# Three bias additions of an attention layer moved from GpSimd's arithmetic to accumulating DMAs

## The chip, the cores and the metric

The kernel runs on one core of a Trainium2 chip. That core has a matrix engine (TensorE, PE in the profile; its weight loads are shown apart as PEld), a vector engine (VectorE, DVE), an activation engine (ScalarE, ACT), a general engine (GpSimd, POOL) and SyncE (SP), which here only issues DMAs. Each engine works through its own queue of instructions in order, and waits on semaphores for the others. The metric is the device time of one execution in microseconds; the times below are the median and the extremes of three executions, and one further execution that the hardware profiler recorded.

## The reference, cut to what matters

The program is a network of two layers over x (32 batches of 512 nodes by 256 features) and an integer adjacency adj (32 x 512 x 512). Layer 0 is a graph convolution and a two-branch feed-forward part; the change does not touch it. Layer 1 is an attention over the graph (4 heads of 64) and a "slice token" mixer (8 heads, 64 slices), each with a layer norm ahead of it and a residual addition behind it:

```python
# attention, per batch; W (4, 256, 64)
h = einsum('bnd,hde->bhne', layernorm(x), W)
weight = leaky_relu(mask * (e_src + e_dst))        # one edge type that matters
weight = where(adj == 0, -1e9, weight)
dst = einsum('bhij,bhje->bhie', softmax(weight), h) + bias
out = relu(dst) + h
out = (out - mean) / sqrt(var + eps) * ln_gamma + ln_beta
x = x + out
# mixer, per batch
sw = softmax((xm @ W_slice.T + b_slice) / temp)    # 512 nodes x (8 heads x 64 slices)
st = einsum('bhnc,bhng->bhgc', fx, sw) / (sum of sw)
ot = state-space mixer over the 64 slice tokens (st)
x = x + einsum('bhgc,bhng->bhnc', ot, sw) @ out_w.T + out_b
```

The three biases of the change are `bias` of the attention (gnn_bias), `ln_beta` and `out_b`. All three are rows of 256 numbers, the same for every node.

## The kernel before, in words

Layer 0 runs first, up to about 2390 us of the span; layer 1 takes the rest, up to 4456 us. Layer 1 is one Python generator. For each batch the nodes lie as 128 partitions times NT = 4 node tiles, so a batch's x is a tile of 128 x 1024 numbers, 512 KB.

**Attention of a batch.** `prepare(b)` gathers x by four indirect DMAs on GpSimd's queue (L1154), builds the mask, normalises x into `xn` (statistics on VectorE L1126, L1127, the inverse root on GpSimd, the scaling on ScalarE L1133), and has GpSimd add beta to x (L1167). Then come the transposes of `xn` and, for each of the four node tiles t, a matmul into a PSUM bank `hp` (L1180). From that bank ScalarE makes `mine` (L1183), the exponential weight of each source node, kept as the 65th column of `hv` (L1184), `other` (L1185), and the copy `ht` of the values (L1186). After all four tiles GpSimd forms the values `hv = ht + abias` (L1189), VectorE multiplies them in place by the weight (L1202), and a small transpose `minep` (L1193) sends `mine` through DRAM to be spread over the partitions as `own` (DMAs at L1198 and L1200). `attention(b)` then forms the weights `att` on VectorE (L1213), multiplies them with `hv` on TensorE (`avp` L1249 for the values, `adp` L1254 for the sums of the weights), copies and transposes both back, and divides: `av = bp * rs` (L1275). Because the weight column sums to the divisor, a bias that is in every value comes out of the division unchanged.

`norm(b, av)` finishes a batch in three parts, which are resumed between the turns of the next batch's attention: first `av = max(av, 0) + ht` (L1290), the mean and its subtraction, and the squares on ScalarE; then the variance, GpSimd's power (L1300) and gamma; then the scaling by the inverse root and `x += av` (L1304).

**Mixer of a pair of batches.** `mixer(g)` takes GB = 2 batches. `slices(b, …)` normalises x again into `x4` (L1133), transposes it, has GpSimd add out_b to x (L1328), and for four node tiles makes logits `lgp` (L1335), their exponential `sw` on ScalarE (L1336) and the softmax on VectorE: times a constant (L1337), row sums (L1340), reciprocal (L1341), scaling (L1342). `yTp` (L1347) multiplies x4 with the finished `sw`, and `swp` (L1352) transposes `sw`. `tokens` and `scan` work on the 64 tokens of both batches. `unslice` multiplies back (`outp` L1567), VectorE adds to x (L1569) and SP stores it.

**What sets the order.** The attention of the batches ahead is woven into the mixer by a pace written by hand: each `yield` of the mixer pays credit (`PACE`, built from `TURNS + STEPS`), and for every whole credit the attention advances by one `yield`. Inside it, `prepare(b+1)` is woven into `attention(b)`, STEPS against TURNS. A scheduler then gives each engine its queue by its own costs and due times, so the order on an engine is not quite that of the program; the buffers (two of `hv`, `ht`, `other`; four PSUM banks called `any`, shared by hp, lgp, yTp, swp, outp and the rest) add waits of their own.

The lines that set it:

```python
PACE = 1.04 * GB * (TURNS + STEPS) / WANTED
...
if unfinished and i != 2:
    next(unfinished[0], None)
    yield
    if i > 2:
        unfinished.pop()
...
yield from woven(attention(b), TURNS - 4, nxt, STEPS)
```

Of the kernel before, what the change touches and what calls it, by code (L numbers as in the profile page):

```python
# [8 lines left out]
F32 = mybir.dt.float32  # L9
# [4 lines left out]
AF = mybir.ActivationFunctionType  # L14
# [5 lines left out]
P = 128  # L20
# [844 lines left out]
def layer1_plain(tc, ident, eps, x2s, ranks, adj, w, out, over, ps):  # L865
# [21 lines left out]
    HE = HO + 1  # L887
    AP = AH // 2
    TURNS = AP * NT + 6
    STEPS = 15  # L890
    WANTED = 68
    AHEAD = 3
    ATT = 2 * (AHEAD + 2) + AP + 1
# [7 lines left out]
    with ExitStack() as ctx:  # L901
# [39 lines left out]
            nc.vector.tensor_scalar(over[:, : 2 * AH], pn[:, : 2 * AH], SMALL, None, ALU.is_gt)  # L941
        yield
        edges = ctile("edges", [P, 2, B * NT])
        abias = const("abias", [P, AH * HO], w["gnn_bias"].rearrange("h e -> (h e)").partition_broadcast(P))
        gamma = const("gamma", [P, AH * HO], w["ln_gamma"].rearrange("h e -> (h e)").partition_broadcast(P))
        beta = const("beta", [P, AH * HO], w["ln_beta"].rearrange("h e -> (h e)").partition_broadcast(P))
        bfx = const("bfx", [P, KC, 1], w["b_fx"].rearrange("(k p o) -> p k o", p=P, o=1))
        bfx_eps = ctile("bfx_eps", [P, KC])
        nc.vector.tensor_scalar_mul(bfx_eps, bfx[:, :, 0], -1e-5)
        outb = const("outb", [P, D], w["out_b"].partition_broadcast(P))  # L950
        conv_w = const("conv_w", [P, KC, KW], w["hy_conv_w"][:DI].rearrange("(c p) k -> p c k", p=P))
        conv_b = const("conv_b", [P, KC], w["hy_conv_b"][:DI].rearrange("(c p) -> p c", p=P))
        bc_w = const("bc_w", [S, 2, KW], w["hy_conv_w"][DI:].rearrange("(c p) k -> p c k", p=S))
# [194 lines left out]
        def prepare(b):  # L1148

            while b >= AHEAD_X and b - AHEAD_X not in stored:  # L1150
                yield True
            xt = xs[b] = sb.tile([P, NT, D], F32, tag="x", name=f"x{b}", bufs=AHEAD_X)
            for t in range(NT):
                nc.gpsimd.indirect_dma_start(  # L1154
                    out=xt[:, t, :], out_offset=None, in_=x2s[b // SEG],
                    in_offset=bass.IndirectOffsetOnAxis(
                        ap=ranks[:, b * NT + t : b * NT + t + 1].bitcast(U32), axis=0))

            hv = sb.tile([P, NT, AH, HE], F32, tag="hv", name=f"hv{b}")
            xn = hv.rearrange("p t h e -> p (t h e)")[:, : NT * D].rearrange("p (t d) -> p t d", t=NT)  # L1160
            edged = masks(b) if b not in masked else range(3)
            for i, _ in enumerate(edged):
                if i < 3 or b not in masked:
                    yield
                if i == 2:
                    normed(xt, xn, f"c{b}")
                    nc.gpsimd.tensor_add(xt, xt, beta.unsqueeze(1).to_broadcast([P, NT, D]))  # L1167
                    yield
            mask = masked.pop(b)
            xnT = yield from turned(xn, "x3T", f"x3T{b}")  # L1170
            yield


            ht = sb.tile([P, NT, AH * HO], F32, tag="ht", name=f"ht{b}")
            other = sb.tile([P, NT, AH], F32, tag="other", name=f"other{b}")
            mine = sb.tile([P, AH, NT], F32, tag="mine", name=f"mine{b}")
            for t in range(NT):
                ph = psum("any", f"hp{b}_{t}")
                for c in range(DC):
                    nc.tensor.matmul(ph[:, : AH * (HO + 2)], xnT[:, c, t * P : (t + 1) * P], wa[:, c, :],  # L1180
                                     start=c == 0, stop=c == DC - 1)
                d = ph[:, AH * HO : AH * HO + AH]
                nc.scalar.activation(mine[:, :, t], ph[:, AH * (HO + 1) : AH * (HO + 2)], AF.Exp, scale=1.0 - SLOPE)  # L1183
                nc.scalar.activation(hv[:, t, :, HO], d, AF.Exp)  # L1184
                nc.scalar.activation(other[:, t, :], d, AF.Exp, scale=SLOPE - 1.0)  # L1185
                nc.scalar.copy(ht[:, t, :], ph[:, : AH * HO])  # L1186
                yield

            nc.gpsimd.tensor_add(hv[:, :, :, :HO], ht.rearrange("p t (h e) -> p t h e", h=AH),  # L1189
                                 abias.rearrange("p (h e) -> p h e", h=AH).unsqueeze(1).to_broadcast([P, NT, AH, HO]))  # L1190
            yield
            pt = psum("any", f"minep{b}")
            nc.tensor.transpose(pt[: AH * NT, :P], mine.rearrange("p h t -> p (h t)"), ident)  # L1193
            row = sb.tile([AH * NT, P], F32, tag="turned", name=f"turned{b}", bufs=1)
            nc.scalar.copy(row, pt[: AH * NT, :P])
            own_row = dr.tile([AH, N], F32, tag="own", name=f"ownd{b}")
            nc.sync.dma_start(own_row.rearrange("h (t p) -> (h t) p", p=P), row)
            own = [wide("own", f"own{b}_{h}", AH + 1) for h in range(AH)]  # L1198
            for h in range(AH):
                nc.sync.dma_start(own[h], own_row[h].partition_broadcast(P))  # L1200
            for t in range(NT):
                nc.vector.tensor_mul(hv[:, t, :, :HO], hv[:, t, :, :HO], hv[:, t, :, HO:].to_broadcast([P, AH, HO]))  # L1202
            ready[b] = mask, ht, hv, other, own
            yield

# [10 lines left out]
        def attention(b):  # L1216

            mask, ht, hv, other, own = ready[b]
            xt = xs[b]
            av = sb.tile([P, NT, AH, HO], F32, tag="av", name=f"av{b}", bufs=1)  # L1220
            turns = [(q, j) for j in range(NT) for q in range(AP)]

            def begin(b, n):
                q, j = turns[n]
                if (b, 2 * q, j) not in weighed:
                    weigh(b, q, j)

            def back(src, kind):

                dst = psum("pv", f"{kind}{b}")  # L1230
                for t in range(NT):
                    nc.tensor.transpose(dst[:, t * P : (t + 1) * P], src[:, t * P : (t + 1) * P], ident)
                return dst

            for n in range(AHEAD):
                begin(b, n)
            pv = [psum("pv", f"avp{b}_{q}") for q in range(AP)]
            for i, (q, j) in enumerate(turns):
                if i + AHEAD < len(turns):
                    begin(b, i + AHEAD)  # L1240
                elif b + 1 in ready:
                    begin(b + 1, i + AHEAD - len(turns))

                if q + 1 == AP:
                    ends = dict(start=j == 0, stop=j == NT - 1)
                    for p in range(AP):
                        for k in range(2 * HO // HW):
                            h, e = 2 * p + k * HW // HO, k * HW % HO
                            nc.tensor.matmul(pv[p][k * HW : (k + 1) * HW, :], hv[:, j, h, e : e + HW],  # L1249
                                             weighed[b, h, j], **ends)  # L1250
                    if j == 0:
                        pd = psum("pv", f"adp{b}")
                    for h in range(AH):
                        nc.tensor.matmul(pd[h * HW : (h + 1) * HW, :], hv[:, j, h, HO:].to_broadcast([P, HW]),  # L1254
                                         weighed.pop((b, h, j)), **ends)
                yield
                if unfinished and i != 2:
                    next(unfinished[0], None)
                    yield
                    if i > 2:  # L1260
                        unfinished.pop()
            dT = wide("att", f"adT{b}", ATT)
            nc.scalar.copy(dT, pd)
            vT = [wide("att", f"avT{b}_{q}", ATT) for q in range(AP)]
            for q in range(AP):
                nc.scalar.copy(vT[q], pv[q])
            yield
            dt = back(dT, "dp")
            rs = sb.tile([P, NT, AH], F32, tag="rs", name=f"rs{b}")
            nc.vector.tensor_scalar_max(rs, dt.rearrange("p (t h e) -> p t h e", t=NT, h=AH)[:, :, :, 0], 1e-30)  # L1270
            nc.vector.reciprocal(rs, rs)
            for q in range(AP):
                bt = back(vT[q], f"bp{q}_")
                heads = slice(2 * q, 2 * q + 2)
                nc.vector.tensor_mul(av[:, :, heads, :], bt.rearrange("p (t h e) -> p t h e", t=NT, h=2),  # L1275
                                     rs[:, :, heads].unsqueeze(3).to_broadcast([P, NT, 2, HO]))
                yield
            unfinished.append(norm(b, av))

        unfinished = []  # L1280
# [37 lines left out]
        def slices(b, j, yT, rn):  # L1318
# [6 lines left out]
            normed(xt, xn, f"d{b}")  # L1325
            yield 5
            xnT = yield from turned(xn, "x4T", f"x4T{b}", 1)
            nc.gpsimd.tensor_add(xt, xt, outb.unsqueeze(1).to_broadcast([P, NT, D]))  # L1328
            sw = sb.tile([P, NT, DI], F32, tag="sw", name=f"sw{b}", bufs=1)
            swT = sb.tile([P, KC, N], F32, tag="swT", name=f"swT{b}")  # L1330
            yield 2
# [908 lines left out]
```

## Time and profile before

| | us |
|---|---|
| median of three executions | 4460.33 |
| lowest, highest | 4456.45, 4473.15 |
| the profiled execution's own time | 4459.08 |
| its span | 4456.4 |
| TensorE busy in it | 3922.0 |
| VectorE busy | 3347.2 |
| ScalarE busy | 2291.6 |
| GpSimd busy | 1718.8 |
| mean granted TensorE clock (share of full speed) | 0.948 |

The profiled execution lies 2.7 us of time outside of its span (4459.08 − 4456.4). A group of instructions in the profile is written as line, engine, operation, out<-in, shape, count, then total busy time and the mean duration of one in nanoseconds, then the idle time of that engine just before them with what ended it. Times in waits are totals over the stretch asked for, with how often and the longest. In layer 1 a pair of batches takes 126.3 us between 2460 and 4230 us (14 pairs); there are 16 pairs.

### The profile page before, as it was taken

How to read it: one execution, taken by the hardware profiler on the slowest of the kernel's cores; microseconds unless marked ns; L12 is line 12 of the kernel's file. 1: busy time of each engine (PE TensorE's matmuls, PEld its weight loads, DVE VectorE, ACT ScalarE, POOL GpSimd, SP SyncE). 2: the span in 40 equal slices, each digit the busy share in tenths (PEclk: the TensorE clock that was granted, in tenths of full speed). 3: DMA queues.
4: the chain of work that ended last, by engine and by line, in shares of the span. 5: the costliest groups of instructions: out<-in, count | busy, mean ns of one | idle time of the engine just before them, and what ended most of it. 6: DMA issues, size and time to landing. Idle time of an engine off the chain costs nothing.

```text
span 4456.4 us, 57911 instructions
## 1 busy us (share of the span) xinstructions
PE 3922.0 (88%) x20311; PEld 2470.6 (55%) x20311; DVE 3347.2 (75%) x7008; ACT 2291.6 (51%) x4756; POOL 1718.8 (39%) x2036
## 2 busy tenths in 40 slices
PE   5568898899988999888997899999999999999987
PEld 4454565566656656545554455555555555555555
DVE  6668887897788987877766777767677877778763
ACT  3345565566564665556654544544545444454433
POOL 2357644664446644454314232332222232332220
PEclk8679999999999999989998999999999999999998
DMA  5546543664436543564422111111111111111100
GB/s 133 160 144 223 190 130 122 210 200 139 156 117 213 187 147 129 162 201 167 138 81 67 36 53 57 56 48 58 51 43 42 53 55 55 58 48 58 41 15 16
DMA packets 235107, 474.21 MB, mean 106 GB/s; under 512 B 38299, under 2 KB 114075, under 8 KB 234804
## 3 DMA queue, kind: packets, MB, share of 16 engines
q0 software_dynamic: 98688, 315.94, 22.2%
q1 hardware_dynamic: 136116, 154.46, 11.0%
q8 instruction: 162, 2.65, 0.2%
q14 instruction: 141, 1.16, 0.1%
HBM read 413.16 MB, written 57.16 MB: 106 GB/s over the span
## 4 chain that ended last, share of the span: by engine, by line
DVE 34%; PE 32%; DMA 11%; issue 9%; POOL 9%; ACT 5%; SPq 0%; POOLq 0%; DVEq 0%; ACTq 0%
DVE att L1213 5%; DVE acc L637 4%; PE clsp L623 3%; PE avp L1249 3%; PE po L652 3%; PE gatep L623 3%; DMA rows<-table,xs 2%; PE yTp L1347 2%; DVE sw L1337 2%; DVE sw L1342 2%; DVE best L598 2%; DMA rows<-table,tops 2%; DVE sst L1340 2%; DMA best<-table,xs 2%; PE xp L1400 1%
## 5 line engine op out<-in xcount | busy, mean ns | idle before, releaser
L623 PE MATMUL clsp<-xnT,wc 128*128 128x512 f32 x1024 | 520.8, 627 | 49.7 <-ACT cls L625 37.6
L623 PE MATMUL gatep<-xnT,wg 128*128 128x512 f32 x1024 | 499.8, 607 | 10.5 <-ACT gate L625 7.7
L652 PE MATMUL po<-wd,acc 128*128 128x256 f32 x2048 | 455.4, 381 | 6.1 <-DVE acc L641 3.8
L1213 DVE SCALAR_TENSOR_TENSOR att<-own,other,mask 128x512 f32<-128x512 f32 x512 | 392.9, 796 | 79.0 <-DMA own<-ownd 79.0
L652 PEld LDWEIGHTS po<-wd,acc 128*128 128x128 f32 x2048 | 388.3, 191 | 72.1 <-issue 9.2
L598 DVE SCALAR_TENSOR_TENSOR best<-rows,xs,best 128x1024 f32<-128x1024 f32 x212 | 274.4, 1295 | 121.9 <-ACT best L592 76.4
L637 DVE SCALAR_TENSOR_TENSOR acc<-past,fld,acc 128x512 f32<-128x512 f32 x448 | 345.7, 775 | 24.9 <-ACT past L636 16.9
L632 ACT ACTIVATE acc<-tz,fld 128x512 f32<-128x512 f32 x256 | 198.8, 777 | 269.3 <-PE tz L630 240.1
L623 PEld LDWEIGHTS gatep<-xnT,wg 128*128 128x128 f32 x1024 | 196.0, 196 | 252.3 <-issue 197.9
L636 ACT ACTIVATE past<-tz,fld 128x512 f32<-128x512 f32 x448 | 291.4, 693 | 68.1 <-DVE acc L637 66.6
L1347 PE MATMUL yTp<-sw,x 128*128 128x512 f32 x512 | 264.6, 655 | 64.3 <-DVE sw L1342 59.6
L595 POOL DMA_INDIRECT rows<-table,xs x212 | 249.5, 1177 | 171.6 <-DVE best L598 119.0
L1249 PE MATMUL avp<-att,hv 128*32 128x512 f32 x2048 | 298.9, 607 | 5.6 <-DVE att L1213 5.6
L623 PEld LDWEIGHTS clsp<-xnT,wc 128*128 128x128 f32 x1024 | 181.5, 198 | 188.1 <-issue 111.8
L434 PE MATMUL pm<-h,adj 128*128 128x258 f32 (+1 forms) x1024 | 181.2, 324 | 99.9 <-DVE keep L427 33.7
L1300 POOL TENSOR_TENSOR mu<-mu,eps 128x16 f32<-128x16 f32 x32 | 111.6, 3487 | 391.1 <-DVE mu L1299 391.0
L1335 PE MATMUL lgp<-wsl,x4T 128*128 128x512 f32 x512 | 242.8, 613 | 15.7 <-ACT sw L1336 6.8
L1154 POOL DMA_INDIRECT x<-x2s,ranks x128 | 135.9, 1062 | 298.1 <-DVE att L1213 148.1
L625 ACT ACTIVATE gate<-gatep,fld 128x512 f32<-128x512 f32 x256 | 175.5, 685 | 142.6 <-PE gatep L623 123.8
L553 POOL DMA_INDIRECT xs<-rows_of,order x128 | 156.1, 1219 | 221.5 <-DVE acc L637 100.8
L1567 PE MATMUL outp<-v,swT 128*128 128x256 f32 x1024 | 227.6, 381 | 0.0
L625 ACT ACTIVATE cls<-clsp,fld 128x512 f32<-128x512 f32 x256 | 176.1, 688 | 93.9 <-PE clsp L623 55.6
(599 smaller groups left out, 8978.1 us busy)
## 6 DMA issues: line engine op xcount, KB each, us to landing
adj<-in_adj POOLq DMA_DIRECT2D x128, 256.0 KB
ai<-in_adj SPq DMA_DIRECT2D x128, 256.0 KB
own<-ownd SPq DMA_DIRECT2D x128, 256.0 KB
rows_of<-keep SPq DMA_DIRECT2D x32, 550.0 KB
x<-in_x SPq DMA_DIRECT2D x32, 512.0 KB
x2s<-xs SPq DMA_DIRECT2D x32, 512.0 KB
out<-x SPq DMA_DIRECT2D x32, 512.0 KB
rows<-table,xs POOLq DMA_INDIRECT x212
```

Of the source, the lines that this page charges most:

```text
L595: nc.gpsimd.indirect_dma_start(out=row, out_offset=None, in_=table, in_offset=bass.IndirectOffsetOnAxis(ap=idxs[:, k : k + 1].bitcast(U32) ...
L598: nc.vector.scalar_tensor_tensor(m, row, vals[:, k : k + 1], m, ALU.add, ALU.max)
L623: nc.tensor.matmul(pf, wf[:, c, f * P : (f + 1) * P], xnT[:, c, :], start=c == 0, stop=c == DC - 1)
L625: nc.scalar.activation(o, pf, fn, bias=fld[:, f, bf : bf + 1], scale=1.0 if fn == AF.Gelu else 0.5)
L636: nc.scalar.activation(r, z, AF.Relu, bias=fld[:, f, AT + b : AT + b + 1])
L637: nc.vector.scalar_tensor_tensor(y, r, fld[:, f, CH + b : CH + b + 1], y, ALU.mult, ALU.add)
L652: nc.tensor.matmul(po[:, i, :], acc[f][:, t * P : (t + 1) * P], wd[:, f, :], start=f == 0, stop=f == FC - 1)
L1213: nc.vector.scalar_tensor_tensor(e, own[h], other[:, j, h : h + 1], mask[:, j, :], ALU.max, ALU.mult)
L1249: nc.tensor.matmul(pv[p][k * HW : (k + 1) * HW, :], hv[:, j, h, e : e + HW], weighed[b, h, j], **ends)
L1335: nc.tensor.matmul(pf, xnT[:, c, t * P : (t + 1) * P], wsl[:, c, :], start=c == 0, stop=c == DC - 1)
L1347: nc.tensor.matmul(py, xn[:, t, c * P : (c + 1) * P], sw[:, t, :], start=t == 0, stop=t == NT - 1)
L1567: nc.tensor.matmul(po[:, :D], swT[:, k, t * P : (t + 1) * P], v[:, k, :], start=k == 0, stop=k == KC - 1)
```

## The change

The three SBUF constants `abias`, `beta` and `outb` go. A DRAM tile `added` of three rows, each the bias row four times (4 KB), is filled by three DMAs on SP. `add_rows` issues from GpSimd's queue a DMA that reads one such row for each of the 128 partitions and adds it to the tile that stands there: 128 rows of 4 KB, 512 KB. It takes the place of GpSimd's additions of beta (L1167) and out_b (L1328). The attention's bias is no longer put into the values: right after ScalarE's exponential of a node tile (which now comes ahead of `mine`), VectorE multiplies the values straight from the PSUM bank by the weight and writes `hv` (after: L1191 and L1192), one tile at a time; the bias is accumulated onto the divided result `av` after the last division, and `norm` reads it after that. The yield behind the old L1189 goes (STEPS 14), and the three parts of `norm` run in turns 1, 2 and 4 where they ran in 0, 1 and 3.

```diff
-    STEPS = 15
+    STEPS = 14
...
-        abias = const("abias", [P, AH * HO], w["gnn_bias"].rearrange("h e -> (h e)").partition_broadcast(P))
+        added = dr.tile([3, NT, D], F32, tag="added", name="added", bufs=1)
+        for i, row in enumerate((w["gnn_bias"].rearrange("h e -> (h e)"), w["ln_beta"].rearrange("h e -> (h e)"),
+                                 w["out_b"])):
+            nc.sync.dma_start(added[i], row.partition_broadcast(NT))
+        added = added.rearrange("i t d -> i (t d)")
+        ABIAS, BETA, OUTB = range(3)
+
+        def add_rows(dst, i):
+
+            nc.gpsimd.dma_start(dst, added[i].partition_broadcast(P), accum_op=ALU.add)
+
...
-        beta = const("beta", [P, AH * HO], w["ln_beta"].rearrange("h e -> (h e)").partition_broadcast(P))
...
-        outb = const("outb", [P, D], w["out_b"].partition_broadcast(P))
...
                     normed(xt, xn, f"c{b}")
-                    nc.gpsimd.tensor_add(xt, xt, beta.unsqueeze(1).to_broadcast([P, NT, D]))
+                    add_rows(xt.rearrange("p t d -> p (t d)"), BETA)
                     yield
...
                 d = ph[:, AH * HO : AH * HO + AH]
+                nc.scalar.activation(hv[:, t, :, HO], d, AF.Exp)
+                nc.vector.tensor_mul(hv[:, t, :, :HO], ph[:, : AH * HO].rearrange("p (h e) -> p h e", h=AH),
+                                     hv[:, t, :, HO:].to_broadcast([P, AH, HO]))
                 nc.scalar.activation(mine[:, :, t], ph[:, AH * (HO + 1) : AH * (HO + 2)], AF.Exp, scale=1.0 - SLOPE)
-                nc.scalar.activation(hv[:, t, :, HO], d, AF.Exp)
                 nc.scalar.activation(other[:, t, :], d, AF.Exp, scale=SLOPE - 1.0)
                 nc.scalar.copy(ht[:, t, :], ph[:, : AH * HO])
                 yield
 
-            nc.gpsimd.tensor_add(hv[:, :, :, :HO], ht.rearrange("p t (h e) -> p t h e", h=AH),
-                                 abias.rearrange("p (h e) -> p h e", h=AH).unsqueeze(1).to_broadcast([P, NT, AH, HO]))
-            yield
             pt = psum("any", f"minep{b}")
...
-            for t in range(NT):
-                nc.vector.tensor_mul(hv[:, t, :, :HO], hv[:, t, :, :HO], hv[:, t, :, HO:].to_broadcast([P, AH, HO]))
             ready[b] = mask, ht, hv, other, own
             yield
...
-                if unfinished and i != 2:
+                if unfinished and i not in (0, 3):
                     next(unfinished[0], None)
                     yield
-                    if i > 2:
+                    if i > 3:
                         unfinished.pop()
...
                 yield
+
+            add_rows(av.rearrange("p t h e -> p (t h e)"), ABIAS)
             unfinished.append(norm(b, av))
...
             xnT = yield from turned(xn, "x4T", f"x4T{b}", 1)
-            nc.gpsimd.tensor_add(xt, xt, outb.unsqueeze(1).to_broadcast([P, NT, D]))
+            add_rows(xt.rearrange("p t d -> p (t d)"), OUTB)
```

## The prediction

> **What bounds the kernel now.** I read the page's busy shares and slices first, then the waits and windows of layer 1, then one pair of batches in the timeline.
>
> ```profile
> PE 3922.0 (88%) x20311; PEld 2470.6 (55%) x20311; DVE 3347.2 (75%) x7008; ACT 2291.6 (51%) x4756; POOL 1718.8 (39%) x2036
> PE   5568898899988999888997899999999999999987
> PEclk8679999999999999989998999999999999999998
> ```
>
> In layer 1 (the second half of the slices) TensorE is at 9 of 10. The window of one pair says the same, and that 10 of its 127 us are idle:
>
> ```profile
> core 0: us, PE busy (x) PEld busy (x) DVE busy (x) ACT busy (x) POOL busy (x), PEclk, DMA share, GB/s
> 2968.00:3095.00 127.00, 117.03 (x766) 70.05 (x766) 91.25 (x198) 61.23 (x158) 36.61 (x28) 0.97 0.16 51
> ```
>
> GpSimd is busy for 37 of 127 us, so taking arithmetic from it gives nothing by itself. What counts is who waits for it. From the groups and the waits of layer 1:
>
> ```profile
> L1189 POOL TENSOR_TENSOR hv<-ht,abias 128x1024 f32<-128x1024 f32 x32 | 80.2, 2506 | 81.2 <-ACT ht L1186 81.2
> L1328 POOL TENSOR_TENSOR x<-x,outb 128x1024 f32<-128x1024 f32 x32 | 75.8, 2370 | 126.8 <-ACT x L1133 125.9 <-PE x4T3p L1142 0.8
> L1202 DVE TENSOR_TENSOR hv<-hv 128x256 f32<-128x256 f32 x128 | 46.6, 420 | 177.5 <-POOL hv L1189 177.5
> ...
> PEld yTp L1347 <- DVE sw L1342: 105.1, 64, 3.8
> DVE att L1213 <- DMA own<-ownd: 79.0, 15, 7.3
> PE yTp L1347 <- DVE sw L1342: 59.6, 36, 3.0
> ```
>
> VectorE stands still for 177.5 us behind GpSimd's `hv`; it is in order, so the softmax `sw` behind L1202 stands with it, and TensorE's `yTp` waits for that softmax. The chain of waits and VectorE's and TensorE's timelines show it:
>
> ```profile
> 2998.64 2.38 POOL x L1328
> 3001.02 2.76 issue
> 3003.78 0.04 POOLq L1167
> 3003.82 2.36 POOL hv L1189
> ...
> 2979.68 2.55 DVE L1342 TENSOR_TENSOR sw<-sw,sst 128x512 f32<-128x512 f32 x1
> 3006.20 1.10 DVE L1202 TENSOR_TENSOR hv<-hv 128x256 f32<-128x256 f32 x3 [7.64 <-POOL hv L1189]
> 3013.50 3.52 DVE L1213 SCALAR_TENSOR_TENSOR att<-own,other,mask 128x512 f32<-128x512 f32 x2
> ...
> 2989.03 3.70 PE L1347 MATMUL yTp<-sw,x 128*128 128x512 f32 x8 [2.10 <-DVE sw L1342]
> 3019.89 7.57 PE L1347 MATMUL yTp<-sw,x 128*128 128x512 f32 x10 [2.98 <-DVE sw L1342]
> ```
>
> Two more things stand here. L1342 usually takes 0.68 us and a pair of L1213 1.41; 2.55 and 3.52 are where GpSimd's addition of beta runs at 2979.29 and 3013.33: 1.9 and 2.1 us lost to it. And the ten matmuls behind the 2.98 us idle take 0.76 us each, the eight behind 2.10 us 0.46. The clock says why:
>
> ```profile
> 3020.00:3022.00 2.00, 2.00 (x3) 0.97 (x4) 2.00 (x5) 0.00 (x0) 0.00 (x0) 0.50 0.00 0
> 3024.00:3026.00 2.00, 2.00 (x3) 0.67 (x2) 2.00 (x3) 0.00 (x0) 0.00 (x0) 0.50 0.00 0
> 3026.00:3028.00 2.00, 2.00 (x11) 1.22 (x10) 1.35 (x2) 0.50 (x2) 0.00 (x0) 1.00 0.00 0
> ```
>
> After 2.98 us idle TensorE works some 6 us at half clock, which costs 3 us more; after 2.10 us it did not. So a pair loses 0.47 + 2.10 + 2.98 idle and 3.0 by the clock, 8.6 us, at this one wait: 16 pairs, 137 us. That is the most that can be won there.
>
> **The change part by part.**
>
> *L1189 and the wait for it.* Gone. The multiplies (128 of 0.42 us) stay; those from a PSUM bank are priced by L1569, the addition with a PSUM input: 417 ns. They wait for one exponential on ScalarE, not for four tiles and 2.5 us of GpSimd. VectorE regains up to 177.5/31 = 5.7 us a batch, 11.4 a pair.
>
> *What is late next.* `minep` stands behind hp directly and ahead of yTp in TensorE's new order, so `own` is sent some 5 us earlier; its wait (79.0/15 = 5.3 us a pair) should mostly go. Against that, in the first batch of a pair four multiplies in a row (1.7 us) and an `att` that needs `own` stand ahead of most of the other batch's softmax, and ScalarE's `mine` now waits for VectorE's multiply (same bank), so ScalarE and VectorE take turns over four tiles. Each turn adds at most one multiply, 4 × 0.42 = 1.7 us a batch, at least 0. I take 1 us on VectorE's path, 2 a pair.
>
> *Beta and out_b.* 2.4 us of GpSimd becomes the issue of a DMA: by the nearest rows 0.57 (its 256 KB loads of adj) to 1.06 us (its gathers). Nobody reads x soon: `x += av` follows a whole attention later, the outp additions a whole scan later. The cover is tens of us, the price 0. The two blocked instructions give back 2.1 + 1.9 = 4.0 us of VectorE a pair. Behind these issues stand, on GpSimd's queue, the normalisation's power and the next gathers; the issue waits for the same ScalarE step as the old addition and is 1.3 us or more shorter, so they come no later.
>
> The Trainium skill has this block as a rule ("SBUF — State Buffer", section "Who interferes with whom"): a VectorE instruction with two SBUF inputs and a GpSimd one that reads SBUF exclude each other for the whole instruction; 3.52 against 1.41 us agrees. The same page's Summary speaks against this change: it would hide a DMA under VectorE's work only when the descriptors do not come from GpSimd, whose writing of them VectorE's fast modes can starve. The gathers are such DMAs: 942 ns least, 956 median, 2227 most of 128, between VectorE's instructions. So here starving is rare; were every issue 2.2 us, the sum would be as with the old additions.
>
> *The bias on `av`.* New, and the one with an exposed wait: the first step of norm (L1290, after: L1297) needs the landing, and VectorE is in order. No row shows an accumulating DMA. Bounds: four `own` copies (1 MB) moved in the windows at 88, 219, 381, 291 and 70 GB/s, 4.5 us, so 512 KB takes 2.25; a gather on GpSimd's queue shows its first bytes 1.4 us after its issue began and is used about 0.5 after its last: 1.4 + 2.25 + 0.5 = 4.2 us. If the bytes standing there must be read as well, twice the data: 6.4. At the gathers' rate (78 to 131, mean 105 GB/s) 5.0 + 1.9 = 6.9, at 78 GB/s 8.6. I take 6.4, because the destination must be read somehow, and keep 4.2 to 8.6.
>
> The Trainium skill ("DMA: Bandwidth & Descriptors", section "Anatomy of one DMA — SWDGE (gpsimd) path") gives 2.0 us and 436 GB/s for a copy, by which 512 KB would be 3.2 us (an estimate); it has no rate for accumulating. Taken at that, there would be no exposure at all.
>
> Cover in the new order of VectorE: between the last division and norm's first step lie, in a pair's first batch, eight `att` (0.66 each) and 0.7 of small ones, 6.0 us; in the second, five `att` and two outp additions (0.42), 4.2 us. At 6.4: 0.4 + 2.2 = 2.6 us of VectorE idle a pair. At 4.2: 0. At 8.6: 2.6 + 4.4 = 7.0. In the second place two more outp additions are queued behind L1297; they free the banks for the next outp, so TensorE can stand there for up to the same 2.2 us, or 1.5 if it has a matmul group left. With no cover each batch would pay the full landing, 12.8 us a pair.
>
> *Rest.* Three small DMAs ahead of layer 1 run beside layer 0: 0. The store of out waits for a DMA instead of GpSimd: hidden. The last batch has no work to lie over: about 5 us once.
>
> **Sum.** VectorE a pair: −11.4 (hv) −4.0 (blocks) −4 (own, of 5.3) +2 (turns) +2.6 (landing) = −15 us of waits, on an engine that has 92 of 127 us of work. TensorE is the bound, so only its 8.6 us count: at best all gone, less 1.5 to 2.2 at outp. Since the softmax still stands behind `att` and four multiplies, I take half of the 8.6, 4.3 us a pair (the idle under the clock's threshold, at least, gives the 3.0 back): 16 × 4.3 = 69, less 5 at the end. From the profiled execution: 4459 − 69 + 5 = 4395; the median is 1.3 above that execution: 4396, which I round up to 4400.
>
> **Rivals.**
>
> *(a) Slower: the landing outlasts its cover.* Place: L1297 of the pair's second batch. At 9.6 us (8.6 and a gather's issue ahead of it on GpSimd's queue) VectorE stands 5.4 us there and 3.6 at the first; TensorE, out of banks, stands about 5, passes the 2.1-to-2.98 us beyond which the half clock comes, and pays 3.0 more: 8 a pair, and the softmax of the batch after is as late as now (none of the 4.3 won): 16 × 4 (half of it hidden) to 8 = +64 to +128, 4525 to 4590. It decides where TensorE's idle reaches 2.9 us: landing 4.2 + 2.9 = 7.1 us or more. For it: the slow end of the bounds; the issue can wait behind GpSimd's power (3.5 us mean) or gathers (four of 1.06). Against: three of the four bounds lie below.
>
> *(b) Same: the wait changes its name.* yTp waits as long, for a softmax now behind `att` and `own` or ScalarE's turns. 2.98 us must only stay above the threshold: 4460 ± 20.
>
> *(c) More:* the yTp waits vanish and no place at outp idles: −8 a pair, 4459 − 128 + 5 = 4336. TensorE's 117 busy us at 0.97 clock allow it.
>
> *(d) It does not do what it says:* the waits go, but TensorE is simply full, and what it no longer waits for at yTp it waits for at hp or avp. That gives (b)'s time.
>
> **How the numbers follow.** Forecast (4365 to 4438) 0.40, (c) and between 0.20, (b) and (d) 0.12, (a) 0.28. Faster 0.60, same 0.12, slower 0.28; the bound is 0.5%, 22 us, about what a measurement of this kernel can tell from no change. The range goes from 4330 (c) up into (a), to 4530, where some 13% lie beyond; the forecast's own range is 4365 to 4438.
>
> **What would show it.** Right: no `hv` wait in VectorE's list; the yTp waits under half of 105.1 and 59.6; no second run of matmuls at clock 0.50 behind yTp; the accumulates landing in about 6.4 us. Wrong: VectorE waiting for DMA at L1297 for over 2.9 us a time, TensorE waiting at outp, a clock of 0.50 in a new place, or GpSimd's issues at 2 us and more.

## The result, and the profile after

The change makes the kernel slower: 4517.64 us (median of four, 4516.56 to 4519.62) against 4458.39; ratio 1.013, interval 1.0104 to 1.0156. The profiled execution has a span of 4517.5 us, 61.1 more than before. Cut at the first `rnp` of each pair, 14.3 us of that lie before the first pair's, 14 pairs of layer 1 take 127.9 us each in place of 125.0 (41.1 together), and 5.7 are in the tail. Of the 14.3, 7.5 are already there when layer 1's first transposes start; such marks lay at 2385 to 2404 us in the profiles of this study, and at 2398 in one kernel without any accumulating DMA (e12 below), so I do not count that part as the change's.

The waits of layer 1 in the kernel after, all engines (columns: total us, times, longest):

```profile
DVE av L1297 <- DMA av<-added: 30.7, 20, 4.9
...
PEld yTp L1354 <- DVE sw L1349: 26.6, 45, 2.0
```

and TensorE's alone:

```profile
PE maskp L1092 <- DVE mask L1093: 55.2, 9, 7.1
PE minep L1200 <- ACT mine L1194: 21.4, 15, 2.3
PE lgp L1342 <- DVE mvc L1135: 19.8, 4, 5.1
```

The wait for `hv` behind GpSimd is gone, and that of yTp for the softmax fell from 105.1 to 26.6 us: the waits that were forecast to go are gone. (VectorE now waits 63.0 us for ScalarE's exponential instead, at L1192.) Two new waits have come. Norm's for the landing is 30.7 us, 2 us a pair. The larger one is behind the outp additions, ahead of maskp or lgp, 4.7 to 9.1 us in each of the 14 pairs. The chain of waits shows one such place (start, us, what):

```profile
3104.09 5.06 DMA av<-added
...
3109.25 1.23 DVE av L1297
...
3112.29 2.93 DMA out<-x
...
3116.00 1.08 POOL x L1162
```

VectorE's timeline there (in brackets the idle before and what ended it):

```profile
3109.25 1.23 DVE L1297 SCALAR_TENSOR_TENSOR av<-av,ht 128x1024 f32<-128x1024 f32 x1 [1.49 <-DMA av<-added]
...
3123.16 0.43 DVE L1134 BATCH_NORM_STATS2 stc<-x 128x6 f32<-128x256 f32 x1 [3.82 <-DMA x<-x2s,ranks]
```

and TensorE's:

```profile
3126.60 0.58 PE L1092 MATMUL maskp<-identb,a 128*128 128x128 bf16 x4 [5.58 <-DVE mask L1093]
```

The accumulation lands 5.06 us after its issue begins; norm waits 1.49 us for it, and norm stands ahead of outp additions. So the store of x starts at 3112.29, the gathers into that buffer at 3116.00, VectorE stands 3.82 us for one of the gathers, and the mask behind it makes TensorE idle 5.58 us. Then comes the clock (a window; PE busy is first, the granted clock is the third number from the end):

```profile
3126.00:3129.00 3.00, 2.40 (x7) 1.36 (x7) 1.91 (x4) 0.00 (x0) 2.79 (x4) 0.50 0.17 51
```

Counted over the 14 pairs, TensorE idles 10.3 us a pair (8.8 before) and is busy 117.6 (116.2), with an idle of over 2.7 us in all 14 (in 9 before).

### The profile page after: what moved, and what is told of

Its sections match the earlier page's. It is cut to its first block, busy times and chain, and to the rows that moved or that the text cites. A ratio compares the mean times of both kernels' runs of the same rounds, so it can differ in the third digit from the quotient of the medians.

```text
span 4517.5 us, 57832 instructions
## 1 busy us (share of the span) xinstructions
PE 3935.4 (87%) x20311; PEld 2478.8 (55%) x20311; DVE 3286.2 (73%) x7008; ACT 2302.9 (51%) x4756; POOL 1575.0 (35%) x2036
## 4 chain that ended last, share of the span: by engine, by line
PE 41%; DVE 23%; DMA 13%; issue 9%; POOL 7%; ACT 6%; SPq 0%; another core or an unknown queue 0%; DVEq 0%; POOLq 0%; ACTq 0%
DVE acc L637 4%; PE yTp L1354 4%; PE lgp L1342 4%; PE avp L1254 4%; PE clsp L623 3%; PE po L652 3%; PE gatep L623 3%; DMA av<-added 2%; DVE best L598 2%; DMA rows<-table,xs 2%; DMA rows<-table,tops 2%; POOL x L1162 2%; PE adp L1259 2%; PE oTp L1542 2%; PE hp L1188 1%
## 5 line engine op out<-in xcount | busy, mean ns | idle before, releaser
L1218 DVE SCALAR_TENSOR_TENSOR att<-own,other,mask 128x512 f32<-128x512 f32 x512 | 359.2, 741 | 7.2 <-DMA own<-ownd 7.1
L595 POOL DMA_INDIRECT rows<-table,xs x212 | 248.7, 1173 | 176.0 <-DVE best L598 123.9
L1342 PE MATMUL lgp<-wsl,x4T 128*128 128x512 f32 x512 | 265.0, 666 | 31.2 <-DVE mvc L1135 19.8
L1354 PE MATMUL yTp<-sw,x 128*128 128x512 f32 x512 | 231.0, 597 | 8.2 <-DVE sw L1349 4.5
L1162 POOL DMA_INDIRECT x<-x2s,ranks x128 | 148.3, 1158 | 237.8 <-DMA out<-x 110.7
L434 PEld LDWEIGHTS pm<-h,adj 128*128 128x128 f32 x1024 | 149.1, 210 | 127.3 <-issue 70.2
```

The source lines that it names most:

```text
L434: nc.tensor.matmul(pm[:, : c1 - c0], a[:, i, t * P : (t + 1) * P], h[:, i, c0:c1], start=i + c0 == 0, stop=i + 1 == NT and c0 > 0)
L595: nc.gpsimd.indirect_dma_start(out=row, out_offset=None, in_=table, in_offset=bass.IndirectOffsetOnAxis(ap=idxs[:, k : k + 1].bitcast(U32) ...
L1218: nc.vector.scalar_tensor_tensor(e, own[h], other[:, j, h : h + 1], mask[:, j, :], ALU.max, ALU.mult)
L1342: nc.tensor.matmul(pf, xnT[:, c, t * P : (t + 1) * P], wsl[:, c, :], start=c == 0, stop=c == DC - 1)
L1354: nc.tensor.matmul(py, xn[:, t, c * P : (c + 1) * P], sw[:, t, :], start=t == 0, stop=t == NT - 1)
```

## The experiments

Every ratio is to the kernel before on the same chip; the kernel before itself had medians from 4449 to 4469 us in these comparisons, so I go by ratios. One per cent is 44.6 us at 4458. "Idle" and "busy" are TensorE's in the profile, us a pair over 14 pairs, and "long" is how many of the 14 have an idle of over 2.7 us. The change's new order, called the weave below, has two parts: "yield" (the yield behind the old L1189 removed, STEPS 14) and "turns" (norm in turns 1, 2, 4). e5, e11, e1 and e13 leave out the attention's bias.

| | kernel | median us | ratio (interval) | idle | busy | long |
|---|---|---|---|---|---|---|
| | before | 4458 | 1 | 8.8 | 116.2 | 9 |
| | after | 4517.6 | 1.013 (1.0104–1.0156) | 10.3 | 117.6 | 14 |
| e4 | rows alone | 4374.1 | 0.9788 (0.9767–0.981) | 5.1 | 113.9 | 0 |
| e10 | beta's row alone | 4371.8 | 0.9823 (0.9806–0.9839) | 5.0 | 113.9 | 0 |
| e5 | e4 + values from the bank | 4372.5 | 0.9806 (0.9783–0.9829) | 4.8 | 113.7 | 0 |
| e11 | e5 − yield | 4421.7 | 0.994 (0.9923–0.9956) | 6.6 | 115.5 | 5 |
| e1 | e11 + turns 1, 2, 4 | 4493.6 | 1.0057 (1.0035–1.0078) | 8.1 | 118.6 | 14 |

The line from e4 through e5, e11 and e1 to the kernel after adds one part at a time.

**First round: is it the landing, or the order?** From the chain above I took the order for the cause: norm ahead of the outp additions.

e1 leaves the attention's bias out:

```diff
-            add_rows(av.rearrange("p t h e -> p (t h e)"), ABIAS)
             unfinished.append(norm(b, av))
```

> The kernel after, without the accumulation of the attention's bias onto av (left out: that bias, which is all zeros in these inputs). Theory 'order': the loss is that norm of a pair's second batch now stands ahead of that pair's outp additions on VectorE, so the store of x, the gathers that reuse its buffer, and the mask behind them are late. The queue of this kernel still has norm there, so it stays slow: 4490 to 4518 us, with an idle of 4 to 6 us of TensorE a pair ahead of maskp or lgp. Theory 'landing': the wait of norm for the accumulated bias is the cause; without it 4455 us or less, and no such idle.

4493.64 us, ratio 1.0057: a loss without any landing. A long idle stays in each of the 14 pairs, but at another place than I expected: 3 stand ahead of lgp (7.6 to 9.1 us), and 11 (3.3 to 4.2 us) ahead of a transpose `x4T` that waits for VectorE's outp addition. The chain of waits shows how one of these comes about:

```profile
2985.28 2.96 DMA out<-x
...
2989.01 1.08 POOL x L1162
...
2994.12 2.95 POOL mu L1306
...
2997.09 1.23 DVE av L1309
2998.31 0.34 DVE x L1575
...
2998.70 1.12 PE x4T8p L1150 x4
```

GpSimd stands 15.45 us for the store before it can issue the gathers (L1162); its power `mu` is behind them in its queue; the last part of norm waits 4.81 us for that power (L1309); and the pair's last outp addition (L1575) is behind norm on VectorE.

e2 puts norm back into turns 0, 1 and 3:

```diff
-                if unfinished and i not in (0, 3):
+                if unfinished and i != 2:
...
-                    if i > 3:
+                    if i > 2:
```

> The kernel after with one edit: the parts of norm run in turns 0, 1 and 3 again. In its queue the pair's first four outp additions stand ahead of the second batch's divisions and norm, as before the change. Theory 'order': the store and the gathers are in time again, the idle of 5 to 6 us a pair goes: 4410 to 4460 us, although L1297 now has only about 2 us of cover and waits longer for the landing (60 us or more in all against 30.7). Theory 'landing': the shorter cover costs more, 4517 us or more.

4500.64, ratio 1.0072 (1.0045–1.0099): only 0.6% better than after, and norm waits longer for the landing:

```profile
DVE av L1297 <- DMA av<-added: 70.8, 32, 5.0
```

Neither theory alone fits. e3 gives x a sixth buffer:

```diff
-    AHEAD_X = 2 * GB + 1
+    AHEAD_X = 2 * GB + 2
-    ATT = 2 * (AHEAD + 2) + AP + 1
+    ATT = 2 * (AHEAD + 2) + AP
```

> The kernel after with six buffers of x in place of five (and one buffer of att less, 12 for 13, to make room), so that the gathers of a new batch do not wait for the store of the batch two pairs back. Theory 'order': the chain outp addition, store, gather, statistics, mask is cut at the store: 4420 to 4470 us, no VectorE wait of 3 us and more for gathers. Theory 'landing': the same landing is waited for, 4500 to 4520 us.

4554.32, ratio 1.0187 (1.0162–1.0211), slower than everything else. Both expectations missed it. The extra buffer also lets the attention run ahead at another place, and there is one att buffer less, and its gathers still wait 111.3 us in all for the store (110.7 in the kernel after), so it says little about the store.

e4 does the part of the rows alone, on the kernel before:

```diff
-                    nc.gpsimd.tensor_add(xt, xt, beta.unsqueeze(1).to_broadcast([P, NT, D]))
+                    add_rows(xt.rearrange("p t d -> p (t d)"), BETA)
...
-            nc.gpsimd.tensor_add(xt, xt, outb.unsqueeze(1).to_broadcast([P, NT, D]))
+            add_rows(xt.rearrange("p t d -> p (t d)"), OUTB)
```

> The kernel before with one part of the change alone: ln_beta and out_b added by accumulating DMAs; values, attention bias, order of norm as before. Theories 'order' and 'landing' alike: nothing waits for these two, and VectorE is no longer blocked by GpSimd's additions (4 us a pair on VectorE): 4410 to 4460 us. Rival 'traffic': 1 MB more of DMA a batch slows the gathers and own, then 4470 us or more here too.

4374.05 us, ratio 0.9788: 2.1% faster than before, more than either theory said, with the whole computation done. The change contains a gain of some 95 us and gives back more. Its waits of layer 1:

```profile
DVE hv L1211 <- POOL hv L1198: 176.0, 31, 8.6
...
PEld yTp L1356 <- DVE sw L1351: 51.9, 55, 1.8
```

and its TensorE timeline at two yTp groups:

```profile
3006.85 4.56 PE L1356 MATMUL yTp<-sw,x 128*128 128x512 f32 x10 [0.88 <-DVE sw L1351]
...
3126.95 4.56 PE L1356 MATMUL yTp<-sw,x 128*128 128x512 f32 x10 [0.73 <-DVE sw L1351]
```

VectorE still waits 176.0 us for GpSimd's `hv`, just as before, and yet the idle ahead of yTp's ten matmuls is 0.73 to 0.88 us where it was 2.98, and they take 4.56 us where they took 7.57. The 2.1 us that went are as much as att lost to beta's addition (3.52 against 1.41), and the half clock went with them: a window as long as a pair of before has the clock at 1.00.

```profile
2970.00:3096.00 126.00, 118.92 (x798) 71.01 (x799) 92.33 (x208) 65.24 (x169) 33.47 (x31) 1.00 0.30 76
```

**Second round: values, weave, landing.** e5 adds the values from the bank to e4, and keeps the yield and the turns of before:

```diff
+                nc.scalar.activation(hv[:, t, :, HO], d, AF.Exp)
+                nc.vector.tensor_mul(hv[:, t, :, :HO], ph[:, : AH * HO].rearrange("p (h e) -> p h e", h=AH),
+                                     hv[:, t, :, HO:].to_broadcast([P, AH, HO]))
                 nc.scalar.activation(mine[:, :, t], ph[:, AH * (HO + 1) : AH * (HO + 2)], AF.Exp, scale=1.0 - SLOPE)
-                nc.scalar.activation(hv[:, t, :, HO], d, AF.Exp)
...
-            nc.gpsimd.tensor_add(hv[:, :, :, :HO], ht.rearrange("p t (h e) -> p t h e", h=AH),
-                                 abias.rearrange("p (h e) -> p h e", h=AH).unsqueeze(1).to_broadcast([P, NT, AH, HO]))
             yield
```

> The kernel of e4 (rows by DMA) plus the values made from the PSUM bank right behind the exponential (ScalarE's new order too); GpSimd's addition L1189 goes, the yield behind it stays, norm in turns 0, 1, 3; the attention's bias is left out. Its VectorE queue around outp is that of before. Theory 'weave' (the removed yield and the moved turns put norm among the outp additions and the gathers late, whatever makes the values): 4340 to 4385 us, faster than or level with e4. Rival 'values' (ScalarE and VectorE taking turns at the bank, minep waiting for mine, cost what was lost): 4430 us or more.

4372.54, level with e4. So the 176 us of VectorE's wait for `hv`, less what the turns at the bank cost, were worth nothing that can be measured. The wait has not wholly gone: in e5 VectorE waits 81.0 us for ScalarE's exponential in its place.

e6 adds only the weave to e4 (yield removed, STEPS 14, turns 1, 2, 4), with GpSimd's values of before.

> The kernel of e4 (values as before, by GpSimd's addition) plus only the weave of the change: the yield behind L1189 removed, STEPS 14, norm in turns 1, 2 and 4. Theory 'weave': most of the loss of e1 against e4 comes back, 4460 to 4500 us, with an idle of over 2.7 us of TensorE in nearly every pair behind the outp additions. Rival 'values': 4365 to 4390 us as e4.

4469.23, ratio 1.0025 (1.0013–1.0038): 2.4% over e4. The weave alone takes back the whole gain.

e7 adds to e4 only the accumulation onto av, in the old weave:

```diff
+            add_rows(av.rearrange("p t h e -> p (t h e)"), ABIAS)
             unfinished.append(norm(b, av))
```

> The kernel of e4 plus the accumulation of the attention's bias onto av ahead of norm (that bias is then added twice; it is all zeros). Values and weave as before. It prices the landing by itself. Theory 'weave': after minus e1 was 24 us, so 4375 to 4405 us, with some 30 to 70 us of VectorE's waits for av. Rival 'landing': with norm's wait ahead of the softmax, 4430 us or more.

4510.69, ratio 1.0108 (1.0078–1.0138): 3.2% over e4, 137 us by the medians. I had expected at most 31 there. Its wait at norm is 2.8 us each time:

```profile
DVE av L1300 <- DMA av<-added: 90.0, 32, 5.2
POOL av L954 <- DVE av L1284: 199.8, 30, 15.5
```

The second line is a wait that I had not looked for: the issue itself stands in GpSimd's queue until the last division, and the inverse roots and the power behind it stand with it. VectorE's wait for the inverse root of the attention's normalisation (`shiftc`) is 58.8 us here and 29.1 in e4.

e8 is the whole change with the weave undone (e2 with the yield back and STEPS 15).

> The whole change with its weave undone: rows and attention bias by accumulating DMAs, values from the bank, but the yield ahead of minep kept, STEPS 15 and norm in turns 0, 1 and 3. Theory 'weave': 4350 to 4400 us, well below both kernels. Rivals 'values' and 'landing': 4470 us or more. e2, which had the turns but not the yield, took 4500.6.

4489.14, ratio 1.0067 (1.0043–1.0091): 2.6% over e5, which lacks only the landing. So "weave" alone falls too: each of the two by itself undoes the gain. The trace of e8 gives the landing, over accumulations onto x and av alike:

```profile
DMA to landing us min/median/max: 4.8/5.2/11.2
```

**Third round: what of the landing, which addition, which part of the weave.** e9 issues e7's third accumulation at the same place, but onto x:

```diff
-            add_rows(av.rearrange("p t h e -> p (t h e)"), ABIAS)
+            add_rows(xt.rearrange("p t d -> p (t d)"), ABIAS)
```

> The kernel of e7 with the third accumulation issued at the same place, of the same size, but onto x, which nobody reads soon, in place of av (the row is all zeros, so x stays). Theory 'wait': e7's 136 us over e4 are norm's wait for the landing; without the wait 4365 to 4395 us. Rival 'traffic': the issue on GpSimd's queue and 512 KB more a batch are the cost; then 4440 us or more.

4399.55, ratio 0.9879 (0.9858–0.99). So 2.3 of e7's 3.2% go when the destination is x. Two waits went together, norm's for the landing and GpSimd's for the division, and no run parts them. The 0.9% that stay are not issue and traffic alone either, for the accumulations onto one x now wait for each other on GpSimd's queue:

```profile
POOL x L954 <- DMA x<-added: 147.3, 28, 7.2
```

e10 takes beta's row alone; out_b stays with GpSimd.

> The kernel before with ln_beta alone added by an accumulating DMA; out_b stays GpSimd's addition. Theory 'block': the gain of e4 comes from GpSimd's additions that stop VectorE's softmax and att, and beta's is the one that meets them (2.1 and 1.9 us a pair in the profile of before): 4370 to 4400 us. Rival: GpSimd's queue got shorter and out_b's addition is what held hv up: 4430 us or more.

4371.77, ratio 0.9823, where the intervals of e10 and e4 just touch: nearly the whole gain is beta's addition, and whether out_b's has the other 0.2 to 0.4% they do not tell. Its wait for `hv` is still 169.6 us.

e11 is e5 with the yield removed and STEPS 14:

```diff
-    STEPS = 15
+    STEPS = 14
...
-            yield
             pt = psum("any", f"minep{b}")
```

> The kernel of e5 with the yield behind the old L1189 removed and STEPS 14, norm still in turns 0, 1, 3; the attention's bias is left out. In its queue norm of the second batch stands behind the pair's first four outp additions but ahead of the last three. It splits the weave. Theory 'turns': turns 1, 2, 4 put norm ahead of the first four additions and so the gathers late, the yield matters little: 4365 to 4400 us. Rival 'yield': 4440 us or more.

4421.68, ratio 0.994 (0.9923–0.9956): between the two expectations. The yield costs 1.3%, the turns (e1 less e11) 1.2%.

e12 leaves out the additions of beta and out_b.

> The kernel before with the additions of ln_beta and out_b left out (both all zeros), nothing in their place; everything else as before. If accumulating DMAs whose landing nobody waits for are free, it is level with e4: 4360 to 4385 us. If they cost something hidden, it is faster than e4 by more than 15 us.

4360.53, ratio 0.9799 (0.9782–0.9815), within e4's interval: two accumulations of 512 KB a batch that nobody waits for cost nothing that can be measured here.

**Fourth round: does the path through the store explain the turns?** e13 changes the credit around the outp additions in e1, so that the pair's first four stand ahead of norm:

```diff
-            yield 2
+            yield 0
             for j in range(GB):
                 unslice(g * GB + j, sws[j], v[:, j])
-                yield 2
+                yield 4 if j == 0 else 2
```

> The kernel of e1 (the change without the attention's bias) with one edit of the mixer's credit: no credit to the attention ahead of the first unslice of a pair (0 for 2), 4 for 2 behind it. In VectorE's queue the pair's first four outp additions now stand ahead of norm of the second batch; in e1 they stand behind its first steps. Theory 'store': the idle of e1 behind the outp additions comes from the late store and the late gathers; 4400 to 4450 us and fewer than half of the 14 idles above 2.7 us. Rival: it is the load of norm beside the start of the next pair, wherever the additions stand; 4475 us or more.

4506.17, ratio 1.0092 (1.0068–1.0117), no faster than e1. The long idles fell from 14 to 9, but idle (8.8 us a pair) and busy (118.7) are no less: other idles took their place, as TensorE's waits show (first two lines).

```profile
PE maskp L1092 <- DVE mask L1093: 28.9, 11, 3.8
PE yTp L1353 <- DVE sst L1347: 21.0, 10, 3.2
POOL x L1162 <- DMA out<-x: 109.5, 7, 15.9
```

The last line shows that the edit did not take the store off the path: GpSimd's gathers wait 109.5 us for it, as against 146.0 in e1, 17.0 in e11 and 2.4 in e5. So e13 neither proves the path through the store nor refutes it.

e14 and e15 try the whole change with the yield kept, all credit behind the second unslice (`yield 0`, `yield 0`, `yield 6`), and norm in turns 1, 2, 3 and 1, 2, 4.

> The whole change, with the yield kept (STEPS 15), norm in turns 1, 2 and 3, and all of the credit around unslice (6) paid behind the second one. The additions of outp of both batches stand ahead of norm of the second one, and the covers of the landing are 4.0 and some 4.2 us. Theory 'landing plus store': the wait at norm is about 1 us a batch, the gathers are in time; 4385 to 4440 us. Rival: the landing costs its 100 us whatever the cover; 4475 us or more.

> As e14 with norm in turns 1, 2 and 4, as in the change: covers 6.0 and some 3.3 us, the outp additions of both batches ahead of norm of the second. Theory 'landing plus store': 4385 to 4450 us, against 4517.6 of the change. Rival: turns 1, 2, 4 are dear wherever the outp additions stand; 4475 us or more.

4513.76, ratio 1.0116 (1.0086–1.0145), and 4475.42, ratio 1.0021 (1.0008–1.0034). e15 is 1.1% better than the change, but it keeps the yield too, which cost 1.3% above, so what the moved credit did is not shown; it is still 2.2% behind e5. In e14 norm's wait for the landing is down to 34.2 us (90.0 in e7), as its theory had it, and the time is no better for that. No version that waits for the landing came below the kernel before. The fastest full version is the rows alone (e4), or only beta's (e10).

## Why the prediction was wrong, by its own steps

The sign was wrong: 4400 was forecast, and the time came out near rival (a), slower (4525 to 4590). (a)'s place is right, but its condition, a landing of 7.1 us or more, was not met, and in the change's own order the landing is 0.7 of the 3.2% that the change loses against e5. That 4517.6 still lies inside the range, to 4530, is luck: it was drawn that far for (a). Two steps failed above all: the gain was credited to `hv`, and the new order was taken to cost nothing. Step by step:

- *"L1189 and the wait for it": the mechanism was wrong.* I took VectorE's 11.4 us a pair behind `hv` for what delays the softmax. e5 against e4 turns that wait into a shorter one (81.0 us, for ScalarE) and moves nothing; e4 and e10 keep it (176.0 and 169.6 us) and have the gain. A long wait of an engine that is not the bottleneck can be time it has to spare.
- *Beta and out_b: the right reading, priced on the wrong engine.* The 1.9 and 2.1 us of blocked VectorE were in my sum as 4.0 us of VectorE, and TensorE's gain as half of 8.6 us for all causes together. Alone they gave 2.1%: the pair went from 125.0 to 118.9 us, 3.7 less idle and 2.4 less busy, the latter with a granted clock that rose from 0.98 to 1.00. By 16 pairs that is 98 us, against my 69 for all. That beta's addition is the cause, but for a few tenths of a per cent, is shown by e10; that it acts by blocking VectorE is read from the rows (2.55 against 0.68, 3.52 against 1.41) and fits the 2.98 that became 0.73 to 0.88. The whole trace agrees: under beta's 32 additions in the kernel before, 28 instructions of the softmax and of att run over 0.3 us longer than their median, 58.9 us in all, and in e4 one such instruction is left (2.0 us). It was not tried apart from the shorter queue of GpSimd. The Trainium skill's rule on this ("SBUF — State Buffer", "Who interferes with whom") was in the prediction; by these runs it was the term that mattered most.
- *The bias on av: the landing was right, its price not.* It lands in 5.06 to 5.2 us, between 4.2 and 6.4. The 2.6 us of VectorE a pair that I foresaw are 30.7/15.5 = 2.0 in the kernel after. I counted TensorE's share as 1.5 to 2.2 us a pair and gave the wait a threshold of 7.1 us. By the runs the same accumulation costs 2.6% in the old weave (e8 less e5, 7.3 us a pair), 1.3% without the yield (e2 less e11) and 0.7% in the new turns (after less e1). So it costs well below my threshold, with waits of 1.5 to 3 us at norm; the chain above shows the mask and the statistics behind that wait coming late. What I did not have at all is the wait of the issue on GpSimd's queue for the last division, 199.8 us in e7 and 218.6 in the kernel after; its share of the price is not shown.
- *The step that I left out: the weave.* I read the new turns and the missing yield only for the cover that they give the landing, and took the rest of the order for free. Without any landing on av they cost 2.5% (e1 less e5: yield 1.3, turns 1.2), and 2.4% with the old values (e6 less e4). They do what they are paid for, since they cut that accumulation's price from 2.6 to 0.7%, but they cost more than that.

In ratios from before, in the order of the table: rows −2.1, values +0.2, yield +1.3, turns +1.2, landing +0.7, together +1.3%. The last four are differences of the table; where they are smaller than the intervals (values) they are nothing.

*"What is late next"* was wrong for `own`: e5 still waits for it. *ScalarE's and VectorE's turns* show no price in e5, though with the yield gone `minep` waits for `mine`, 21.4 us in the kernel after. *The clock's threshold*, 2.1 to 2.98 us for one idle, was wrong, as the last section shows.

What stays open is how much of the turns' 1.2% runs by which path. The chains of e1 and of the kernel after both begin at the store: gathers that wait for it, and behind them GpSimd's power or the statistics and the mask. Where the turns came in (e11 to e1) the gathers' wait for the store went from 17.0 to 146.0 us. But no run takes that wait away and leaves the turns, so the path is read and not shown. Why the missing yield costs 1.3% is open as well; in e11 the largest new waits of TensorE are minep's for `mine` (14.5 us) and yTp's for the softmax.

## What to carry to other kernels

Before a wait is priced, ask whether its engine had time to spare: shortening the 177 us wait was worth nothing, and two instructions a pair that were blocked for 2 us each, just ahead of the bottleneck, were worth about 2%. An accumulating DMA showed no price where its landing is read long after (e4 against e12), and a price of 0.7 to 3.2% where an engine reads it 2 to 6 us later: split such a change by destination before taking it whole. Ask also what the issue waits for, since everything behind it in its queue waits too. A hand-woven order is a term of the sum of its own; run it alone.

## What the runs showed of the hardware

The half clock needs no single long idle. In every trace here the granted clock changes only at the borders of a grid of 3.41 us, whose place differs from run to run, and what counts is TensorE's idle time in one such stretch, added up. The prediction has an idle of 2.10 us that left the clock alone: the border at 2988.44 cut it into 1.52 and 0.58, and the eight matmuls behind it took 3.70 us. The same kernel has an idle of the same length that lies within one stretch, and there eight take 5.40 (TensorE's timeline, then two stretches of the grid):

```profile
3867.95 5.40 PE L1347 MATMUL yTp<-sw,x 128*128 128x512 f32 x8 [2.10 <-DVE sw L1342]
...
3865.67:3869.08 3.41, 1.31 (x4) 0.66 (x4) 3.41 (x9) 0.00 (x0) 1.28 (x1) 1.00 0.00 0
3869.08:3872.49 3.41, 3.41 (x5) 1.37 (x5) 3.41 (x8) 0.10 (x1) 0.00 (x0) 0.50 0.00 0
```

In e15 an idle of 1.70 us and the first part of one of 0.68 us, with 0.7 us of small transposes between them, fall into one stretch (busy 1.34 of 3.41 us), and the next is at half clock (windows again):

```profile
3083.93:3087.34 3.41, 1.34 (x8) 0.68 (x6) 1.37 (x3) 3.14 (x13) 0.91 (x1) 1.00 0.56 105
3087.34:3090.75 3.41, 3.10 (x14) 3.11 (x15) 0.00 (x0) 0.25 (x1) 0.00 (x0) 0.50 0.49 130
```

Counted over the 17 profiles from 2500 to 4180 us, by the records of TensorE: of the stretches at full clock, all 171 with over 2.0 us of idle are followed by one at half clock, none of the 7402 with under 1.0 us, and 47 of the 450 between. So my threshold of 2.1 to 2.98 us for one idle was the wrong kind of rule. The Trainium skill ("TensorE: Matmul & The Clock Gate", section "Part 1: The HAM clock gate") has the gate watch free-running windows of some 3.4 us, which agrees with the grid; its rule against idle gaps above some 3.4 us is too kind by these counts. It also says ("Part 4: PE-mode transpose") that transposes do not count as busy in the way that matmuls do. These traces do not need that: with transposes counted as idle, only 47 of the 188 stretches with 2.0 to 2.5 us are followed by half clock.

Accumulating 512 KB onto a tile took 5.2 us in the median from issue to landing (e8), 4.8 at least and 11.2 at most: 1 us over my estimate for a copy (4.2), and less than the 6.4 for twice the bytes. Its issue holds GpSimd for 0.87 us in the median (onto av, in the kernel after).
